# Causal stage: one block projected ahead, blocks taken as 0, 2, 3, 1, and zero products beside the first unit's maxima scores

## The chip, the core and the metric

The kernel runs on one core of one Trainium2 chip. A core has five engines with queues of their own: TensorE (PE, matrix products, with its weight loads shown as PEld), VectorE (DVE), ScalarE (ACT), GpSimd (POOL) and SyncE (SP, which issues DMAs here). Each takes its instructions in the order of its queue and waits for others by semaphores. The metric is device time in microseconds of one execution, and the median over runs is compared. TensorE's clock is granted by a throttle; the profile shows it as a share of full speed.

## What is computed

A model of four layers works on one sequence of 2048 tokens of width 128; layers are attention-like or feed-forward blocks, each added to the residual stream. The part that changes is the second attention of layer 0, causal attention with 16 heads of width 8 and rotary embedding. Reduced to what matters:

```python
q, k, v = heads(Wq, bq), heads(Wk, bk), heads(Wv, bv)
q = _apply_rope(q, cos, sin)
k = _apply_rope(k, cos, sin)
att = jnp.einsum('bhqd,bhkd->bhqk', q, k) * (1.0 / np.sqrt(D))
causal = jnp.tril(jnp.ones((T, T), bool))
att = jnp.where(causal[None, None], att, NEG_BIG)
att = jax.nn.softmax(att, axis=-1)
y = jnp.einsum('bhqk,bhkd->bhqd', att, v)
y = y.transpose(0, 2, 1, 3).reshape(B, T, C)
return jnp.einsum('btc,oc->bto', y, Wp) + bp
```

The result goes onto the residual stream, and a mixture-of-experts stage follows.

## The kernel before

Fourteen stages run one after the other (`STAGES`). Each works on the 2048 tokens as four blocks of 512 (`NB`, `BW`). The residual stream `x` stays on the chip. `Core.run` drives the stages as generators: while one stage's `main` runs, a `feed` opens the next stage and runs its first steps, block by block (`blocks`, `early`), as soon as the current stage says that it has room. A block is taken up only when the stage before has finished it: `before.final > b`. The attribute `own` says how many blocks a stage leaves for its own `main`; the first `NB - own` come ahead of it. What of the feed is not done when the stage before ends is run to its end there. The order of instructions on each engine comes from a scheduler that simulates the program, except that products of the Causal stage marked by `in_turn` keep the order in which the program issues them.

The Causal stage (`Attn16`, `Attention`):

- `early(b)` projects a block: layer norm (`normed`, `turned`), values into `at_V` (`project`), keys through `heads("k", b)` and four `slot` products into the transposed keys `at_KT`, one tile for each group of four heads. `heads` multiplies by the weights and by a rotated copy of them, loads the cosine and sine tables of the block (256 KB each, single buffers), multiplies by them on DVE, adds on POOL and splits the result into two parts for precise products. `heads("q", b)` does the same for the queries.
- Before, `own` is 1: blocks 0, 1 and 2 come ahead of the stage's `main`, then `main` projects block 0's queries. Block 3 is projected in steps (`tick`, `need`) between the scores.
- A unit is a pair of a head group g and a query block b; 16 units in the order of blocks 0, 1, 2, 3, four groups each. The last query rows' keys are those of blocks 0 to b, so the work of a unit grows with b + 1.
- `pass_a(u)` finds the row maxima: scores of two heads for 128 queries and up to 512 keys (L829), a mask on the diagonal (L832) and a maximum (L833), both on DVE. At the end of a unit the maxima are transposed (L850), copied (L852) and sent by DMA into the query tile (L854), so that later scores come out with the maximum subtracted.
- `pass_b(u)` computes the transposed scores by key tiles of 128 (L900, with the mask as a product, L903), exponentiates on ACT (L906) and multiplies by the values (L879), accumulating in the one PSUM bank `ps_c`. Beside these stand products with a tile of zeros (L883), which add nothing to the sums.
- The maxima of the next units run ahead of the exponential pass by six pairs of scores (`lead`), so that at a change of block the longer maxima of the new block stand beside the exponentials of the old one.
- `tail` and `out` normalise, project and add to the residual (L948) once all four groups of a block are done; `out` sets `final` to b + 1.

Of the kernel before, what the change touches and what calls it, by code (L numbers as in the profile page):

```python
# [15 lines left out]
BF16 = mybir.dt.bfloat16  # L16
# [5 lines left out]
P = 128  # L22
T = 2048
NT = T // P
NB = 4
# [7 lines left out]
class Core:  # L33
    def __init__(self, ctx, tc, ins):
        self.ctx, self.tc, self.nc, self.ins = ctx, tc, tc.nc, ins
        nc = self.nc
        self.per = ctx.enter_context(tc.tile_pool(name="per", bufs=1))
        self.x = self.per.tile([P, NT, P], F32, name="x")
        self.load_x(ins["x"])
        self.ident = self.per.tile([P, P], F32, name="ident")  # L40
        make_identity(nc, self.ident)
        self.identb = self.per.tile([P, P], BF16, name="identb")
        nc.vector.tensor_copy(self.identb, self.ident)
        self.identr = self.per.tile([P, P], F32R, name="identr")
        nc.vector.tensor_copy(self.identr, self.ident)
        self.ones = self.per.tile([P, P], F32, name="ones")
        nc.vector.memset(self.ones, 1.0)
        self.nhalf = self.per.tile([P, 4], F32, name="nhalf")
        nc.vector.memset(self.nhalf, -0.5)
        self.rev8 = self.per.tile([P, 4, E], F32, name="rev8")  # L50
        for e in range(E):
            nc.vector.memset(self.rev8[:, :, e : e + 1], float(E - e))
        self.neg01 = self.load(self.per, "neg01", (P, 1), ins["neg01"])
        slots = self.per.tile([P, 4, P], F32R, name="slots")
        with tc.tile_pool(name="st0", bufs=1) as st:
            nc.vector.tensor_copy(slots, self.load(st, "slots_raw", (P, 4, P), ins["slots"]))
        self.slots = {"q": (slots[:, 0], slots[:, 1]), "k": (slots[:, 2], slots[:, 3])}
        self.kone = self.load(self.per, "kone", (P, 1), ins["kone"])
        one = self.per.tile([2, 1], F32R, name="ones2")
        nc.vector.tensor_copy(one, self.ones[0:2, 0:1])  # L60
        self.ones2 = one.to_broadcast([2, BW])
        self.wide = self.per.tile([P, BW], BF16, name="wide")
        nc.vector.memset(self.wide, 1.0)
        self.zerob = self.per.tile([P, 32], BF16, name="zerob")
        nc.vector.memset(self.zerob, 0.0)
        self.psum = ctx.enter_context(tc.tile_pool(name="psum", bufs=1, space=PSUM))
        self.shared = {}
# [106 lines left out]
class Stage:  # L174
# [5 lines left out]
    own = 0  # L180
# [382 lines left out]
class Attention(Stage):  # L563
# [3 lines left out]

    pace = 12

    lead = 0.15  # L570

    halve, ahead = True, 0.35
    own = 2
    every = 1

    def start(self):
        self.have, self.count = NB - self.own, 0
        self.left = self.blocks(self.have, NB)

    apart = 4  # L580
# [23 lines left out]
    def units(self, scale):  # L604


        units = [(g, b, 0, 4) for b in range(NB) for g in range(4)]
        if self.halve:
            units[0:1] = [(0, 0, 0, 2), (0, 0, 2, 4)]
        preps = [u[:2] for n, u in enumerate(units) if u[2] == 0][1:]  # L610
        follows = {u: v[:2] for u, v in zip(units, units[1:]) if v[2] == 0}

        def astream():
            for n, u in enumerate(units):
                for p in self.pass_a(u):
                    self.tick()
                    if preps and p > self.ahead and preps[0] == follows.get(u):
                        self.prep(*preps.pop(0))
                    yield n + p
                yield n + 1.0  # L620

        sa = astream()
        pos = 0.0
        lead = lambda n: self.lead if self.lead < 1 else self.lead / self.pairs_of(units[min(int(n), len(units) - 1)])

        def advance(to):
            nonlocal pos
            while pos < to:
                pos = next(sa, 1e9)

        prev, at = iter(()), 0.15
        advance(1.0 + lead(1))
        for n, u in enumerate(units):
            for p in self.pass_b(u, scale):
                advance(min(n + 1 + p + lead(n + 1 + p), len(units)))
                if p > at:
                    next(prev, None)
                    at += self.gap
                yield
            for _ in prev:  # L640
                pass
            prev, at = self.finish(u), 0.15
        for _ in prev:
            pass
# [3 lines left out]
    def finish(self, u):  # L648
        self.tail(u)
        if u[0] == 3 and u[3] == 4:  # L650
            yield
            yield from self.out(u[1])


    pre = None

# [18 lines left out]

    def finish_late(self, u):
        while self.closed != u:
            if u == (3, NB - 1, 0, 4):
                self.later(2)
            else:  # L680
                yield
        yield from Attention.finish(self, u)


class Attn16(Attention):
# [38 lines left out]
    def early(self, b):  # L724
        xn = self.normed(b)
        yield
        ln = self.turned(xn)
        yield
        for _ in self.project(b, ln):
            yield  # L730

    def heads(self, which, b):
# [55 lines left out]
    def main(self):  # L788
        self.start()
        self.wk = self.pool("at_k", 2)  # L790
        self.qhl = self.heads("q", 0)
        self.prep(0, 0)
        self.banks()
        for b in range(self.have):
            add_bias(self.c, self.bo, b)
        self.roomy = True
        yield from self.units(self.scale)

    def prep(self, g, b):
        q = self.wk.tile([P, BW], F32R, name="at_q", bufs=self.NQ)  # L800
        self.slot(q, "q", g, self.qhl)
        if g == 3 and b + 1 < NB:
            self.need(b + 2)
            self.qhl = self.heads("q", b + 1)
        self.qb[(g, b)] = q

    def pass_a(self, u):

        c, nc = self.c, self.c.nc
        g, b, i0, i1 = u
        q, KT = self.qb[(g, b)], self.KT[g]
        mx = self.wk.tile([P, 4, 4, 4], F32, name="at_mx")
        nch = b + 1 if self.causal else 4
        steps = self.steps(u, nch)
        for n, (i, ch) in enumerate(steps):
            nk = P * (4 * b + i + 1) if self.causal else T
            w = min(BW, nk - ch * BW)
            diag = self.causal and ch == nch - 1  # L820
            self.need(ch + 1)
            left = [1, 0]
            while left:
                jj = self.pair if self.pair in left else left[0]
                left.remove(jj)
                pa = self.ps("a", (P, 2, BW))
                for k in range(2):
                    r = rows(2 * jj + k)
                    self.in_turn(nc.tensor.matmul(pa[:, k, :w], q[r, i * P : (i + 1) * P], KT[r, ch * BW : ch * BW + w], start=True, stop=True))  # L829
                if diag:  # L830
                    d = pa[:, :, w - P : w]
                    nc.vector.tensor_tensor(d, d, self.maskb.unsqueeze(1).to_broadcast([P, 2, P]), ALU.add)  # L832
                nc.vector.tensor_reduce(mx[:, i, 2 * jj : 2 * jj + 2, ch], pa[:, :, :w], AX.X, ALU.max)  # L833
                if n == len(steps) - 1 and not left:
                    self.due.append([2, u, self.set_max(lambda j: q[32 * j + 24 : 32 * j + 26], mx[:, :, :, 0:nch], i0, i1)])
                yield (n + 1 - len(left) / 2) / len(steps)

    def set_max(self, to, mx, i0=0, i1=4):
        c, nc = self.c, self.c.nc
# [21 lines left out]
    def pass_b(self, u, scale):  # L861
        c, nc = self.c, self.c.nc
        g, b, i0, i1 = u
        self.turn_due(u)
        q, KT = self.qb[(g, b)], self.KT[g]
# [3 lines left out]
        def av(kt, off, ps, half):  # L869
# [6 lines left out]
            for j in (3, 2, 1, 0):  # L876
                h = 27 * (4 * (g // 2) + j) + 9 * (g % 2)
                start, stop = kt == i0 == g % 2 == half == 0, kt == nkt - 1 and g % 2 == half == 1
                self.in_turn(nc.tensor.matmul(self.acc[32 * j : 32 * j + 32, s], self.V[:, kt, h : h + 32], ps[j][:, s], start=start, stop=stop))  # L879
            z = s if kt == 0 or end < BW else slice(half * BW // 2, (half + 1) * BW // 2)  # L880
            for j in (3, 2, 1, 0):
                if not (kt == nkt - 1 and half):
                    self.in_turn(nc.tensor.matmul(self.acc[32 * j : 32 * j + 32, z], c.zerob, c.wide[:, z], start=False, stop=False))  # L883
            if kt == nkt - 1 and half:
                self.closed = u
            if kt == nkt - 1 and g % 2 == half == 1:
# [48 lines left out]
    def out(self, b):  # L935
        c, nc = self.c, self.c.nc
# [9 lines left out]
            nc.tensor.matmul(po[:, i * P : (i + 1) * P], yT[:, i * P : (i + 1) * P], self.wt["o"], start=True, stop=True)  # L946
        xb = c.xb(b).rearrange("p t d -> p (t d)")
        nc.vector.tensor_tensor(xb, po, xb, ALU.add)  # L948
        self.final = b + 1


class Causal(Attn16):
    pre, causal, rope, halve = "l0b_", True, True, False
    own = 1
    lns = 4
    lnx = 1


class Attn2(Attn16):
    pre, halve, own = "l2b_", False, 1  # L960
# [3 lines left out]
class Filtered(Attn16):  # L964
    pre, halve, own = "l3b_", False, 1
# [341 lines left out]
class Mla(Attention):  # L1307
# [9 lines left out]
    own = 0  # L1317
# [199 lines left out]
    def out(self, b):  # L1517
        c, nc = self.c, self.c.nc
# [12 lines left out]
                nc.tensor.matmul(po[:, s], yT[:, k, s], self.F[:, k, :], start=(k == 0), stop=(k == 1))  # L1531
        xb = c.xb(b).rearrange("p t d -> p (t d)")
        nc.vector.tensor_tensor(xb, po, xb, ALU.add)
        self.final = b + 1


class Ssm(Stage):
# [271 lines left out]
class Hale(Attn16):  # L1809
# [41 lines left out]
    own = 0  # L1851
# [587 lines left out]
```

## Time and profile before

| | |
|---|---|
| runs | 4833.01, 4835.98, 4851.77 us |
| median | 4835.98 us |
| profiled execution | 4842.59 us, its span 4840.6 us |
| mean granted clock | 0.922 |
| Causal stage, first maxima score to last residual addition | 318.2 to 860.9 us |

The costliest groups of the stage, from 300 to 865 us of the profiled execution:

| line, engine, what | count | busy us | mean ns |
|---|---|---|---|
| L833 DVE maxima | 320 | 330.1 | 1062 |
| L906 ACT exponentials | 640 | 305.0 | 532 |
| L879 PE values | 2560 | 207.4 | 401 |
| L900 PE transposed scores | 640 | 181.4 | 505 |
| L829 PE scores for the maxima | 640 | 165.8 | 530 |
| L883 PE zero products | 1216 | 98.6 | 304 |
| L832 DVE masks | 128 | 54.2 | 427 |

Products overlap in the array, so that the busy times of PE's groups add up to more than PE's own. A stretch of the profile is named by its microseconds from the start of the span. In the answers by stretch, the columns are the length, the busy time of PE, PEld, DVE, ACT and POOL with the number of instructions in brackets, the granted clock, the share of the DMA engines and the GB/s moved.

### The profile page before, as it was taken

Reading aid. Unit: us, or ns where it says so; the run is one execution under the profiler, and the core shown is the slowest. Engines: PE = TensorE matmul, PEld = TensorE weight load, DVE = VectorE, ACT = ScalarE, POOL = GpSimd, SP = SyncE. Lnnn points to the kernel's source line nnn. Section 1 sums busy time; section 2 is a strip of 40 time slices with the busy share of each in tenths; the row PEclk is TensorE's granted clock in tenths of the full one; section 3 lists DMA queues with packets and bytes.
Section 4 is the critical chain, followed back from the end, with each engine's and each line's share of the span. In section 5 each row is a group of like instructions: output and inputs, shape, how many; then the busy total and the mean of one; then the engine's idle time right before and its main releaser. Section 6 shows DMA issues by size and latency. Waiting matters only on the chain.

```text
span 4840.6 us, 89173 instructions
## 1 busy us (share of the span) xinstructions
PE 4411.5 (91%) x36388; PEld 2496.4 (52%) x36388; DVE 3713.6 (77%) x5694; ACT 3052.4 (63%) x5570; POOL 947.6 (20%) x826
## 2 busy tenths in 40 slices
PE   6979999988799998799999999989988989999998
PEld 4744444655344443463444457656656634444466
DVE  7867886689666653789999958457768879999777
ACT  4634667775355555356888875345546648888876
POOL 4730000544100000330000013012215600000056
PEclk9966899998699999888999999889998969999999
DMA  1010000000000000000000000112211000000000
GB/s 52 6 45 6 4 2 9 22 1 17 17 14 14 18 14 4 8 1 2 2 2 2 2 4 12 33 50 51 51 48 37 9 8 2 2 2 2 2 20 7
DMA packets 69484, 73.33 MB, mean 15 GB/s; under 512 B 17616, under 2 KB 44102, under 8 KB 69076
## 3 DMA queue, kind: packets, MB, share of 16 engines
q1 hardware_dynamic: 69076, 67.64, 5.0%
q8 instruction: 287, 4.70, 0.4%
q14 instruction: 121, 0.99, 0.1%
HBM read 32.09 MB, written 1.05 MB: 7 GB/s over the span
## 4 chain that ended last, share of the span: by engine, by line
PE 68%; DVE 21%; ACT 5%; issue 3%; POOL 2%; DMA 1%; SPq 0%; POOLq 0%; ACTq 0%; DVEq 0%
PE ps_c L879 15%; PE ps_a L829 10%; PE ps_c L1483 5%; DVE at_mx L833 4%; PE ps_b L900 4%; PE ps_a L1443 3%; PE ps_c L883 3%; PE ps_b L1496 3%; PE ps_b L148 2%; PE ps_a L148 2%; PE ps_a L150 2%; PE ps_b L149 2%; PE ps_a L149 2%; PE ps_b L150 2%; DVE m_hl L455 1%
## 5 line engine op out<-in xcount | busy, mean ns | idle before, releaser
L906 ACT ACTIVATE at_P<-ps_b 128x512 f32<-128x512 f32 (+2 forms) x2688 | 1414.4, 581 | 335.0 <-PE ps_b L900 211.1
L833 DVE TENSOR_REDUCE at_mx<-ps_a 128x2 f32<-128x1024 f32 (+2 forms) x1344 | 1537.7, 1184 | 106.5 <-PE ps_b L900 66.8
L879 PE MATMUL ps_c<-at_P,at_V 128*32 128x256 f32 (+3 forms) x10752 | 868.3, 396 | 7.8 <-ACT at_u L888 7.3
L900 PE MATMUL ps_b<-at_q,at_KT 32*128 32x512 f32 (+2 forms) x2688 | 759.5, 499 | 6.6 <-DMA at_q<-at_mT 5.0
L829 PE MATMUL ps_a<-at_KT,at_q 32*128 32x512 f32 (+3 forms) x2688 | 701.1, 521 | 48.0 <-DVE at_mx L833 45.7
L829 PEld LDWEIGHTS ps_a<-at_KT,at_q 32*128 32x128 f32 x2688 | 267.1, 196 | 497.4 <-issue 338.1
L1444 DVE TENSOR_REDUCE ml_mx<-ps_a 128x2 f32<-128x1024 f32 x256 | 305.4, 1222 | 216.4 <-PE ps_a L1443 215.4
L454 ACT ACTIVATE m_hh<-ps_a,moe_b 128x512 fp32r<-128x512 f32 x512 | 349.8, 689 | 189.1 <-DVE m_h L451 158.0
L455 POOL TENSOR_TENSOR m_hl<-m_h,m_hh 128x512 fp32r<-128x512 f32 x256 | 360.5, 1409 | 541.1 <-ACT m_hh L454 529.3
L1498 ACT ACTIVATE ml_P<-ps_b 128x512 f32<-128x512 f32 (+1 forms) x544 | 272.5, 576 | 231.8 <-PE ps_b L1496 229.7
L879 PEld LDWEIGHTS ps_c<-at_P,at_V 128*32 128x32 f32 x10752 | 215.8, 110 | 359.2 <-issue 181.0
L883 PE MATMUL ps_c<-wide,zerob 128*32 128x256 bf16 x5184 | 391.1, 282 | 0.0
L266 POOL TENSOR_TENSOR ln_rs<-ln_ve,nhalf 128x4 f32<-128x4 f32 x56 | 61.8, 1104 | 1650.3 <-DVE ln_ve L264 1641.4
L900 PEld LDWEIGHTS ps_b<-at_q,at_KT 32*128 32x128 f32 x2688 | 326.3, 189 | 73.5 <-issue 44.2
L455 DVE TENSOR_TENSOR m_hl<-m_h,m_hh 128x512 fp32r<-128x512 f32 x256 | 257.1, 1005 | 79.4 <-ACT m_hh L454 77.9
L453 ACT ACTIVATE m_h<-ps_a,moe_b 128x512 f32<-128x512 f32 x320 | 220.6, 690 | 77.1 <-DVE m_hl L455 42.0
L1483 PE MATMUL ps_c<-ml_P,ml_V 128*33 128x512 f32 (+3 forms) x1088 | 257.5, 596 | 2.9 <-ACT ml_P L1498 2.9
L148 PE MATMUL ps_b<-m_hh,moe_w2h 128*128 128x512 f32 x512 | 221.7, 433 | 20.7 <-DVE m_t L475 17.8
L149 PE MATMUL ps_b<-m_hl,moe_w2h 128*128 128x512 f32 x512 | 213.9, 418 | 26.4 <-DVE m_hl L455 20.7
L148 PE MATMUL ps_a<-ln_h,moe_w1h 128*128 128x512 f32 x512 | 218.7, 428 | 10.7 <-ACT m_hh L454 10.6
L883 PEld LDWEIGHTS <-zerob 128*32 128x32 bf16 x5184 | 156.1, 100 | 113.6 <-issue 10.8
L149 PE MATMUL ps_a<-ln_l,moe_w1h 128*128 128x512 f32 x512 | 207.4, 405 | 0.0
(655 smaller groups left out, 7759.7 us busy)
## 6 DMA issues: line engine op xcount, KB each, us to landing
hl_KS<-hl_pkh SPq DMA_DIRECT2D x160, 64.0 KB
moe_w_raw<-in_l0f_W SPq DMA_DIRECT2D x32, 256.0 KB
ml_pad<-ml_QT SPq DMA_DIRECT2D x32, 256.0 KB
moe_w_raw<-in_l3f_W SPq DMA_DIRECT2D x32, 256.0 KB
hl_KS<-hl_pkl SPq DMA_DIRECT2D x80, 64.0 KB
at_pad<-at_q SPq DMA_DIRECT2D x64, 64.0 KB
at_q<-at_mT SPq DMA_DIRECT2D x192, 4.0 KB
at_cosT<-in_cosT SPq DMA_DIRECT2D x8, 256.0 KB
```

The source lines that it names most:

```text
L148: nc.tensor.matmul(out, lh, rh, start=start, stop=False)
L149: nc.tensor.matmul(out, lh, rl, start=False, stop=False)
L454: nc.scalar.activation(hh, ph, AF.Relu, bias=bias)
L455: (nc.gpsimd if f in ((0, 2) if self.spare else MS) else nc.vector).tensor_tensor(hl, h, hh.bitcast(F32), ALU.subtract)
L829: self.in_turn(nc.tensor.matmul(pa[:, k, :w], q[r, i * P : (i + 1) * P], KT[r, ch * BW : ch * BW + w], start=True, stop=True))
L833: nc.vector.tensor_reduce(mx[:, i, 2 * jj : 2 * jj + 2, ch], pa[:, :, :w], AX.X, ALU.max)
L879: self.in_turn(nc.tensor.matmul(self.acc[32 * j : 32 * j + 32, s], self.V[:, kt, h : h + 32], ps[j][:, s], start=start, stop=stop))
L883: self.in_turn(nc.tensor.matmul(self.acc[32 * j : 32 * j + 32, z], c.zerob, c.wide[:, z], start=False, stop=False))
L900: self.in_turn(nc.tensor.matmul(pbs[k][:, off:end], KT[r, kt * P : (kt + 1) * P], q[r, off:end], start=True, stop=not diag))
L906: nc.scalar.activation(p[:, off:end], pbs[k][:, off:end], AF.Exp, scale=scale)
L1444: nc.vector.tensor_reduce(mx[:, i, :, ch], pa, AX.X, ALU.max)
L1483: self.in_turn(nc.tensor.matmul(self.acc[64 * j : 64 * j + m, s], v, ps[k][j][:, s], start=kt + k == 0, stop=kt + k == NT - 1))
```

## The change

Three parts, all in the Causal stage. `own` goes from 1 to 3: only block 0 is projected ahead, and its queries belong to that projection; blocks 1, 2 and 3 are projected between the scores, where each gets its bias addition too (`prepared`). The blocks' units are taken in the order 0, 2, 3, 1; `final` counts up only over blocks that are finished without a gap. And while no unit is closed and no value product is pending, each pair of maxima scores is followed by two products of a 128x128 tile of zeros with a 128x512 tile of ones into `ps_c`; for this the zero tile grows from 32 to 128 columns, and the older zero products use its first 32. In the changed program 32 such products stand in PE's queue, between the score pairs of the first unit and of most of the second. The other stages' order of instructions stays, but for a few neighbours changing places.

```diff
-        self.zerob = self.per.tile([P, 32], BF16, name="zerob")
+        self.zerob = self.per.tile([P, P], BF16, name="zerob")
...
+    order = tuple(range(NB))
...
-        self.have, self.count = NB - self.own, 0
+        self.have, self.count, self.through = NB - self.own, 0, set()
...
-        units = [(g, b, 0, 4) for b in range(NB) for g in range(4)]
+        units = [(g, b, 0, 4) for b in self.order for g in range(4)]
...
+    def over(self, b):
+        self.through.add(b)
+        while self.final in self.through:
+            self.final += 1
...
-            if u == (3, NB - 1, 0, 4):
+            if u == (3, self.order[-1], 0, 4):
...
         for _ in self.project(b, ln):
             yield
+        if b == self.order[0]:
+            self.qhl = self.heads("q", b)
+            yield
...
         self.wk = self.pool("at_k", 2)
-        self.qhl = self.heads("q", 0)
         self.prep(0, 0)
...
-        if g == 3 and b + 1 < NB:
-            self.need(b + 2)
-            self.qhl = self.heads("q", b + 1)
+        if g == 3 and b != self.order[-1]:
+            b1 = self.order[self.order.index(b) + 1]
+            self.need(b1 + 1)
+            self.qhl = self.heads("q", b1)
...
                 nc.vector.tensor_reduce(mx[:, i, 2 * jj : 2 * jj + 2, ch], pa[:, :, :w], AX.X, ALU.max)
+                if self.closed is None and not self.late:
+                    self.warm()
...
+    busy = 0
+
+    def warm(self):
+        if self.busy:
+            pz = self.c.ps("c")
+            for _ in range(self.busy):
+                self.in_turn(self.c.nc.tensor.matmul(pz, self.c.zerob, self.c.wide, start=True, stop=True))
...
-                    self.in_turn(nc.tensor.matmul(self.acc[32 * j : 32 * j + 32, z], c.zerob, c.wide[:, z], start=False, stop=False))
+                    self.in_turn(nc.tensor.matmul(self.acc[32 * j : 32 * j + 32, z], c.zerob[:, 0:32], c.wide[:, z], start=False, stop=False))
...
-        self.final = b + 1
+        self.over(b)
...
 class Causal(Attn16):
     pre, causal, rope, halve = "l0b_", True, True, False
-    own = 1
+    own = 3
     lns = 4
     lnx = 1
+    order, busy = (0, 2, 3, 1), 2
```

The other attention stages keep `order` 0, 1, 2, 3 and `busy` 0.

More of the change, by code (lines that the diff above doesn't have):

```diff
@@ L1533, in out @@
         nc.vector.tensor_tensor(xb, po, xb, ALU.add)
-        self.final = b + 1
+        self.over(b)
 class Ssm(Stage):
```

## The prediction

> **What bounds the kernel now.** I read the page first, then a table of busy time by stretch of the Causal stage (marks: 281.0, where block 0's keys are done; 318.2, the first maxima product; then the moments at which a unit's or a block's maxima are copied out at L852, read off ScalarE's timeline; 856.3, the last unit's copy-out), then short windows of the clock, then the timeline.
>
> ```profile
> PE 4411.5 (91%) x36388; PEld 2496.4 (52%) x36388; DVE 3713.6 (77%) x5694; ACT 3052.4 (63%) x5570; POOL 947.6 (20%) x826
> ...
> PEclk9966899998699999888999999889998969999999
> ```
>
> TensorE (PE) is busy 91% of the span. The stage lies in slices 3 to 8, where the clock row shows its first 6.
>
> ```profile
> 281.00:318.20 37.20, 24.47 (x65) 13.44 (x65) 15.66 (x35) 11.75 (x19) 6.18 (x5) 0.58 0.28 86
> 318.20:340.40 22.20, 14.78 (x55) 7.56 (x54) 19.21 (x38) 4.78 (x8) 1.26 (x1) 0.50 0.07 24
> 340.40:388.00 47.60, 47.14 (x350) 21.55 (x354) 29.41 (x56) 18.97 (x46) 1.27 (x1) 0.50 0.04 13
> 388.00:415.80 27.80, 25.32 (x214) 12.10 (x210) 18.78 (x28) 8.96 (x25) 0.00 (x0) 0.56 0.01 2
> 415.80:503.80 88.00, 84.11 (x828) 39.00 (x828) 68.07 (x126) 48.91 (x104) 3.57 (x3) 0.74 0.03 8
> 503.80:534.40 30.60, 26.68 (x322) 12.49 (x318) 28.56 (x36) 16.94 (x40) 0.00 (x0) 0.97 0.01 2
> 534.40:638.60 104.20, 101.06 (x1214) 46.45 (x1213) 92.92 (x131) 73.71 (x153) 3.39 (x13) 0.91 0.02 5
> 638.60:676.90 38.30, 34.59 (x432) 15.89 (x428) 36.79 (x43) 24.92 (x54) 0.00 (x0) 0.99 0.01 2
> 676.90:813.20 136.30, 135.48 (x1609) 60.37 (x1605) 115.63 (x144) 98.95 (x199) 1.02 (x1) 0.88 0.01 2
> 813.20:856.30 43.10, 42.38 (x554) 19.51 (x547) 0.00 (x0) 35.31 (x75) 0.00 (x0) 1.00 0.07 21
> ```
>
> Columns: length, busy us of PE, weight loads, VectorE (DVE), ScalarE, GpSimd, then the clock. I call these rows S0 to S9; they sum to 575.3. Read four things. S0 holds no attention at all: blocks 1 and 2 and block 0's queries are projected while PE works 24 of 37 us at 0.58. In S2, the rest of block 0, PE is full (47.1 of 47.6) at half clock, and DVE is not (29.4). S3 and S5 are the passages to a longer block, and S5 is nearly all DVE. In S9 the last exponential pass runs alone, DVE empty.
>
> ```profile
> 375.00:380.00 5.00, 5.00 (x56) 2.34 (x54) 4.05 (x6) 1.98 (x6) 0.00 (x0) 0.50 0.01 3
> ...
> 438.15 0.79 PE L829 MATMUL ps_a<-at_KT,at_q 32*128 32x512 f32 x2
> 438.16 0.79 PE L900 MATMUL ps_b<-at_q,at_KT 32*128 32x512 f32 x2
> 438.88 1.08 PE L879 MATMUL ps_c<-at_P,at_V 128*32 128x256 f32 x8
> 439.74 0.44 PE L883 MATMUL ps_c<-wide,zerob 128*32 128x256 bf16 x4
> 440.11 0.71 PE L829 MATMUL ps_a<-at_KT,at_q 32*128 32x512 f32 x2
> ```
>
> The clock is 0.50 from 287.0 to 409.9, again to 440.6, then mostly 1.00. It moves in steps of 3.41 us. A PE without a gap does not lift it: 375 to 380 is full at 0.50. Products over all 128 rows and columns do. I counted, over the whole trace, the 3.41-us steps at 0.50 that hold hardly anything else: filled to 75% or more with such products, 19 of 19 are followed by full clock; filled to 41 to 74%, 13 of 23. At 440.6 it rises after a step of unmasked value products (L879), zero products (L883) and scores on all four row groups together.
>
> The page of the Trainium skill titled "TensorE: Matmul & The Clock Gate", section "What's actually happening", says that one window of about 3.4 us of sustained activity gives full clock, which speaks against the zero products, since PE is already busy after 344. The rows differ, so the measurement decides. If the page's plain rule held, the products would be added work only, and the sum would be that of rival A below.
>
> **The change, part by part.** New stretches, in the new order.
>
> *Start (S0).* Blocks 1 and 2 no longer come ahead of attention. What is left is block 0's queries: 306.2 (first bias product) to 318.2 is 12.0 us, placed at 281. S0 becomes 12, that is 25 less. Nothing is removed: the two projections go into the next stretch. Each issues rope-table loads of 256 KB on SP and one GpSimd add of 1.26 us per rope, in single buffers; GpSimd is 6% busy in S1, so I price both at nothing there. Uncovered, one rope chain is the 2.8 to 3.6 us wait for the cast in S0, three times some 10 us.
>
> *First maxima (S1).* DVE: 19.2 now, plus what leaves S0: 15.7 less four weight splits of the next stage (4 x 0.69) and the query rope's three passes (2.1), so 10.8, together 30. PE at half clock: 14.8, plus 24.5 less some 6.5 for the queries, so 18, plus 32 zero products (two for each of 16 score pairs) of 128x512; the same shape in bf16 takes 0.43 between starts at half clock, 13.7. Together 46.5. The zero products make more than half of a step a full-height product and the projections' weight products add to it, so I take the clock to rise after three steps: 10 us at half, then 36.5/2 = 18, so 28 on PE. DVE then decides: 30 at S1's own share (19.21/22.20) is 35. Ends: 33, and 48 if the clock stays (46.5 over 0.97). The products write the single ps_c bank, which nothing else uses before the first value product on the same engine.
>
> *Rest of block 0 (S2).* Half clock: 47.6. Full clock: PE 23.6, DVE 29.4/0.865 = 34. No zero products are added after the first unit closes, and this work has never lifted the clock by itself, so I take the middle, 41.
>
> *Block 0 to block 2.* 24 wide maxima beside only 4 key tiles: DVE decides as in S5, 28.6 busy of 30.6. I take 32; ends 31 and 36 (half clock).
>
> *Block 2 (S6)* 104.2, with its 17 us at half clock inside; 106, ends 104 and 115. *Block 2 to 3 (S7)* 38.3 and *block 3 (S8)* 136.3 are as before.
>
> *Block 3 to block 1 (new).* The maxima lead by 6 pairs: 6/32 of a unit at block 3, 6/16 at block 1. So S9 is 1.19 units of lone exponential pass in 43.1, 36.2 a unit. The new passage holds 0.19 + 0.62 = 0.81 units, 29.5, and PE also does 16 score pairs of some 0.3: 35, ends 34 and 38.
>
> *Block 1 last (S4).* 88.0 at clock 0.74. At full clock DVE's 68.1 at S6's share (0.892) is 76. It starts warm but has the same masked tiles: 80, ends 76 and 88.
>
> *End (S9).* 1.375 units of 8 tiles, at 36.2/2 = 18.1: 25, ends 24 and 26.
>
> The reordering by itself moves little: each passage costs about the longer of its two halves, and in units of a block's length 1+3+2+6+3+9+4+12+4 = 44 is also 1+3+3+9+4+12+4+6+2. What pays is the start and the clock.
>
> Sum: 12 + 35 + 41 + 32 + 106 + 38.3 + 136.3 + 35 + 80 + 25 = 540.6, against 575.3: 34.7 less. Lower ends: 12+33+34+31+104+38.3+136.3+34+76+24 = 522.6, 52.7 less. Upper ends: 12+48+47.6+36+115+38.3+136.3+38+88+26 = 585.2, 9.9 more. The profiled execution took 4842.6 (span 4840.6), so it would be 4808; the runs' median is 4836.0, so I forecast 4801.
>
> **The rivals.** *A, the zero products do not lift the clock* and are work only: every stretch at its upper end, 4836 + 10 = 4846. For it: 375 to 380, and steps of 59, 66 and 73% full-height products that stayed low. Against it: the 19 of 19, and half of the rest, with ten steps in S1's 35 us to try in.
>
> *B, slower: the half clock is carried into block 2.* The place is the passage to block 2: 24 maxima keep DVE full and PE thin, as in 388 to 415.8, where the clock fell back to 0.50 after one step. Block 2's units are PE-full: S6 has 101.1 of 104.2 at 0.91, 33.7 a unit, which is 61 at 0.50 against 34.7, so 26.6 for each unit that runs low. On top of A, with one unit: 4846 + 27 = 4873. It decides from there; on top of my forecast it takes three units, 34.7 less against 80 more. Against it: block 1 recovered at 440.6 within its first exponential pass, and block 2 has eight unmasked tiles a unit.
>
> *C, the head start is eaten* because the projections' chains queue in order on PE and DVE: S1 at 48 with full clock afterwards, 22 less, 4814. It falls short of what can be told from no change and counts with A.
>
> **How the numbers follow.** Differences under 0.5% (24 us) can't be told from no change. Forecast (24 to 53 less) 0.55; A and C 0.28; B 0.17. The forecast's own range is 4783 to 4812; A, B and C lie beyond it. The range reaches down below the lower ends and up past A, part of B left out: 4775 to 4855. Faster by over 24 us takes the clock to rise in S1 or S2 at least in part: 0.55; same 0.28; slower 0.17.
>
> **What would show it.** First maxima product near 293 instead of 318; the clock at 1.00 within some 10 us after it; the first exponential pass near 328; block 0's maxima done by about 369; DVE empty for some 25 us at the end instead of 46.6; everything after the stage early by the same amount. I am wrong if the clock row is 0.50 throughout 290 to 400, if block 2's first unit shows 0.50, or if the first exponential pass starts no sooner than 340.

## The result, and the profile after

The changed kernel takes 4869.14 us (median of 14 runs, 4848.86 to 4899.49), the kernel before 4840.67 beside it (14 runs). The ratio is 1.0062, 95% interval 1.0046 to 1.0078: slower by some 30 us, where 35 less had been forecast and 4855 was the top of the range. The profiled execution took 4882.1, its span 4880.0, the mean granted clock 0.915 (0.922 before).

From the page of the changed kernel: busy time by engine, and the clock by fortieths of the span.

```profile
PE 4452.2 (91%) x36398; PEld 2512.8 (51%) x36420; DVE 3707.2 (76%) x5694; ACT 3051.3 (63%) x5570; POOL 950.8 (19%) x826
...
PEclk9966896999689999797999999889998969999999
```

PE is busy 41 us more than before, with hardly more instructions. The Causal stage lies in slices 3 to 8 as it did. By stretch, with the columns of the prediction's table (length; busy PE, weight loads, DVE, ACT, POOL; clock); the marks are the first maxima product (300.0), the copies of the maxima, now at L873, and at the end the copy of the last unit's result (L909):

```profile
282.00:300.00 18.00, 11.12 (x30) 6.51 (x30) 9.15 (x23) 6.29 (x11) 4.71 (x6) 0.50 0.43 132
300.00:342.30 42.30, 37.98 (x130) 17.24 (x132) 27.81 (x55) 9.16 (x15) 5.17 (x4) 0.66 0.12 37
342.30:397.40 55.10, 52.98 (x367) 23.59 (x370) 33.01 (x59) 22.11 (x51) 1.27 (x1) 0.50 0.04 12
397.40:439.10 41.70, 33.66 (x246) 15.25 (x242) 28.60 (x35) 9.54 (x28) 0.00 (x0) 0.50 0.01 1
439.10:551.40 112.30, 106.68 (x1184) 49.20 (x1185) 92.58 (x148) 74.30 (x150) 4.59 (x14) 0.86 0.02 7
551.40:590.20 38.80, 35.09 (x436) 15.92 (x432) 36.31 (x43) 24.86 (x53) 0.00 (x0) 0.98 0.01 2
590.20:725.80 135.60, 132.44 (x1612) 59.31 (x1612) 117.96 (x141) 100.17 (x201) 1.28 (x1) 0.92 0.02 4
725.80:766.60 40.80, 40.47 (x401) 16.52 (x393) 20.06 (x28) 26.02 (x53) 0.00 (x0) 0.71 0.01 2
766.60:864.00 97.40, 93.96 (x957) 41.93 (x953) 60.85 (x88) 55.43 (x120) 0.00 (x0) 0.74 0.01 2
864.00:887.50 23.50, 23.39 (x328) 11.31 (x320) 0.00 (x0) 17.38 (x43) 0.00 (x0) 1.00 0.11 36
```

Two marks of the prediction's table are not such copies. 340.4, called the first copy-out, is the first score of the exponential pass (the copy stands at 337.9); 856.3 lies 0.9 us behind the copy of the last result (855.4). That first score comes at 345.5 in the change, and by this mark its second and third stretch are:

```profile
300.00:345.40 45.40, 40.82 (x136) 18.09 (x138) 29.47 (x57) 10.39 (x18) 5.17 (x4) 0.65 0.11 35
345.40:397.40 52.00, 50.14 (x358) 22.74 (x362) 31.35 (x57) 20.89 (x50) 1.27 (x1) 0.50 0.04 12
```

Set against the rows S0 to S9, in the order of the work, with these two for S1 and S2:

| from, to | before | forecast | after |
|---|---|---|---|
| first maxima product at | 318.2 | 293 | 300.0 |
| first score of the exponential pass at | 340.4 | 328 | 345.4 |
| rest of block 0 | 47.6 | 41 | 52.0 |
| passages 0 to 1 and 1 to 2, block 1 in the middle / passages 0 to 2 and 3 to 1, block 1 last | 146.4 | 147 | 179.9 |
| block 2 | 104.2 | 106 | 112.3 |
| passage 2 to 3 and block 3 | 174.6 | 174.6 | 174.4 |
| lone end | 43.1 | 25 | 23.5 |
| stage's last copy-out at | 856.3 | 821.6 | 887.5 |

Of the 25 us that the start was to bring, 18 are there at the first maxima product; at the first exponential score the change is 5 us behind the kernel before. The end is shorter by 20 us, where 18 were forecast; the passages, block 1, block 0 and block 2 take all of it back and 31 more. The other 7 or 8 us by which this execution is longer come behind the stage. Of the three signs by which the prediction was to be wrong two are there: block 2's first unit shows 0.50, and the exponential pass starts later than 340. The third, a clock of 0.50 throughout 290 to 400, is not.

Short stretches show the clock:

```profile
306.00:309.40 3.40, 3.40 (x11) 0.98 (x9) 1.62 (x3) 0.22 (x1) 1.26 (x1) 0.50 0.23 77
309.40:323.10 13.70, 12.03 (x57) 5.49 (x58) 13.03 (x26) 4.14 (x7) 2.64 (x2) 1.00 0.14 41
319.60:323.10 3.50, 1.97 (x12) 0.64 (x10) 3.50 (x8) 0.62 (x1) 1.26 (x1) 1.00 0.29 86
323.10:342.30 19.20, 16.89 (x54) 7.98 (x54) 9.64 (x20) 4.22 (x7) 1.26 (x1) 0.50 0.11 39
...
439.10:463.00 23.90, 22.98 (x155) 10.60 (x153) 11.52 (x15) 10.88 (x20) 0.00 (x0) 0.50 0.01 2
463.00:480.00 17.00, 15.59 (x201) 7.10 (x203) 16.27 (x32) 12.63 (x24) 2.30 (x2) 1.00 0.00 1
```

The clock rises at 309.4, behind a step (306.0 to 309.4) that holds two pairs of zero products and the last weight products of a late block's keys. It stays up for four steps, in which DVE is nearly full (13.03 of 13.70) and sets the pace; in the last of them, the line 319.60:323.10, PE works 1.97 us of 3.50 beside a full DVE. Then it is 0.50 for 140 us, from 323.1 to 463.0, through the whole passage to block 2 and into block 2's first unit: the mechanism of rival B.

### The profile page after: what moved, and what is told of

It is laid out like the page before. It is cut to its first block, busy times and chain, and to the rows that moved or that the text cites. A ratio compares the mean times of both kernels' runs of the same rounds, so it can differ in the third digit from the quotient of the medians.

```text
span 4880.0 us, 89208 instructions
## 1 busy us (share of the span) xinstructions
PE 4452.2 (91%) x36398; PEld 2512.8 (51%) x36420; DVE 3707.2 (76%) x5694; ACT 3051.3 (63%) x5570; POOL 950.8 (19%) x826
## 4 chain that ended last, share of the span: by engine, by line
PE 69%; DVE 20%; ACT 4%; issue 3%; POOL 2%; DMA 1%; SPq 0%; POOLq 0%; ACTq 0%; DVEq 0%
PE ps_c L900 15%; PE ps_a L839 10%; PE ps_c L1505 5%; DVE at_mx L843 4%; PE ps_b L921 4%; PE ps_c L904 3%; PE ps_a L1465 3%; PE ps_b L1518 3%; PE ps_a L148 2%; PE ps_b L148 2%; PE ps_a L150 2%; PE ps_a L149 2%; PE ps_b L149 2%; PE ps_b L150 2%; DVE m_hl L455 1%
## 5 line engine op out<-in xcount | busy, mean ns | idle before, releaser
L843 DVE TENSOR_REDUCE at_mx<-ps_a 128x2 f32<-128x1024 f32 (+2 forms) x1344 | 1540.0, 1184 | 139.8 <-PE ps_b L921 76.9
L927 ACT ACTIVATE at_P<-ps_b 128x512 f32<-128x512 f32 (+1 forms) x2688 | 1414.4, 581 | 352.2 <-PE ps_b L921 224.4
L900 PE MATMUL ps_c<-at_P,at_V 128*32 128x256 f32 (+2 forms) x10752 | 874.6, 399 | 7.8 <-ACT at_u L909 7.3
L921 PE MATMUL ps_b<-at_q,at_KT 32*128 32x512 f32 (+1 forms) x2688 | 763.3, 502 | 6.0 <-DMA at_q<-at_mT 4.3
L839 PEld LDWEIGHTS ps_a<-at_KT,at_q 32*128 32x128 f32 x2688 | 268.8, 197 | 500.4 <-issue 340.4
L900 PEld LDWEIGHTS ps_c<-at_P,at_V 128*32 128x32 f32 x10752 | 216.3, 110 | 361.2 <-issue 184.6
```

The source lines that it names most:

```text
L921: self.in_turn(nc.tensor.matmul(pbs[k][:, off:end], KT[r, kt * P : (kt + 1) * P], q[r, off:end], start=True, stop=not diag))
L927: nc.scalar.activation(p[:, off:end], pbs[k][:, off:end], AF.Exp, scale=scale)
```

## The experiments

Eleven other kernels and the changed one once more, each with runs of the kernel before beside it; none leaves out any part of the computation. The four sets of runs of the kernel before have means between 4841.9 and 4843.5 us. "Own" is the number of blocks that the stage leaves for itself, "zeros" the zero products per pair of maxima scores.

| kernel | own | order | zeros | ratio | 95% interval | half clock, us | at equal half clock, us |
|---|---|---|---|---|---|---|---|
| before | 1 | 0123 | 0 | 1 | | 758 | 4852.8 |
| order_only | 1 | 0231 | 0 | 1.0026 | 1.0010 to 1.0042 | 796 | 4854.7 |
| own_only | 3 | 0123 | 0 | 1.0014 | 0.9989 to 1.0040 | 788 | 4852.1 |
| zeros_only | 1 | 0123 | 2 | 1.0016 | 0.9994 to 1.0039 | 774 | 4856.6 |
| own_zeros | 3 | 0123 | 2 | 1.0018 | 0.9993 to 1.0043 | 777 | 4857.8 |
| own_order | 3 | 0231 | 0 | 1.0001 | 0.9988 to 1.0013 | 764 | 4852.5 |
| order_zeros | 1 | 0231 | 2 | 1.0001 | 0.9983 to 1.0019 | 747 | 4857.5 |
| busy1 | 3 | 0231 | 1 | 1.0040 | 1.0024 to 1.0056 | 803 | 4858.5 |
| the change | 3 | 0231 | 2 | 1.0062 | 1.0046 to 1.0078 | 812 | 4864.6 |
| after_again (the change) | 3 | 0231 | 2 | 1.0077 | 1.0049 to 1.0104 | 822 | 4869.1 |
| dose4 | 3 | 0123 | 4 | 1.0034 | 1.0020 to 1.0048 | 777 | 4864.5 |
| nat_hold | 1 | 0123 | held | 0.9992 | 0.9979 to 1.0005 | 668 | 4877.6 |
| order_hold | 1 | 0231 | held | 0.9979 | 0.9964 to 0.9993 | 644 | 4879.5 |
| own_order_hold | 3 | 0231 | held | 1.0006 | 0.9988 to 1.0024 | 678 | 4880.2 |

The last two columns are worked out from the runs: time at half clock is twice (1 - mean granted clock) times the whole program's span, averaged over a kernel's runs (4 to 14; the kernel before 99). One straight line through the runs of all kernels, with a height for each kernel, has a slope of 0.31 us for each microsecond at half clock; the last column is that height at 790 us. It is a fit and not an experiment: it says that the two go together, not which makes which. The two sets of the change, 4.5 apart in it, show how good it is. For the three "held" kernels, 110 to 150 us away from 790, it is drawn far beyond their own runs.

**One part at a time.** order_only, own_only, zeros_only and own_zeros take the changed kernel and set back these lines:

```diff
-    own = 3
-    order, busy = (0, 2, 3, 1), 2
+    own = 1                            (order_only, zeros_only)
+    order, busy = (0, 2, 3, 1), 0      (order_only)
+    order, busy = (0, 1, 2, 3), 0      (own_only)
+    order, busy = (0, 1, 2, 3), 2      (zeros_only, own_zeros)
```

> Only the order 0, 2, 3, 1 of the change; three blocks ahead as before, no zero products beside the maxima (block 0's queries are projected right behind its keys, ahead of blocks 1 and 2). Theory O (the order is the loss: the 24 maxima of block 2 behind block 0 keep the half clock, and block 1 runs low again at the end): slower than before by 20 to 45 us, with the half clock reaching past the first maxima of block 2 and a passage 0 to 2 of some 40 us. Theory P (the deferred projections are the loss): within 10 us of before. Theory Z (the zero products are the loss): the same.

> Only one block projected ahead; natural order, no zero products. Theory O: faster than before by 5 to 20 us, since the first maxima start some 18 us sooner and half of it is given back. Theory P: slower than before by 15 us or more, with block 0's maxima done later than 388. Theory Z: within 10 us of before.

> Only the 32 zero products beside the first maxima; three blocks ahead, natural order. Theory O and P: within 10 us of before, the clock up for some 10 to 15 us and down again once the products end. Theory Z: slower by 15 us or more.

> The change without its order: one block ahead and the zero products, blocks 0, 1, 2, 3. Theory O: faster than the changed kernel by 25 to 45 us and not slower than before. Theory P or Z: within 15 us of the changed kernel, that is some 15 to 30 us slower than before.

Measured: only the order by itself is slower beyond doubt, by 0.26%, and that at equal half clock is 2 us; it meets 38 us more of half clock. These 13 us are fewer than the 20 to 45 of theory O. The early start and the zero products alone can't be told from no change, and together (own_zeros) they can't either; own_zeros is some 20 us faster than the change, less than O's 25 and more than the 15 of P and Z. So none of the three theories has its part that carries the loss, and the head start is worth nothing that can be measured even in the old order. The three single excesses add up to 0.56%, close to the change's 0.62; the pairs, below, show that this sum is a coincidence. No run sets all three parts back at once, so the rest of the edit (block 0's queries projected ahead of the stage, the wider zero tile) has no price of its own.

zeros_only shows the zero products at their weakest. The columns are as above, then L857, the zero products, by itself, with 30 of the 32 in the first stretch:

```profile
313.80:348.70 34.90, 33.87 (x97) 12.68 (x96) 21.64 (x40) 5.36 (x9) 1.26 (x1) 0.50 0.04 16
348.70:396.00 47.30, 46.89 (x353) 21.20 (x356) 29.15 (x55) 19.34 (x47) 1.27 (x1) 0.50 0.04 13
```

```profile
313.80:348.70 34.90, 15.59 (x30) 2.05 (x30) 0.50 0.04 16
```

From the first maxima product on, PE is full (33.87 of 34.90), nearly half of that is zero products over the whole array (15.59), and the clock is 0.50 throughout.

That it rose in the change seems to have been a matter of half a microsecond. own_zeros has the same products there, its second pair of zero products at 306.76 and the change's at 306.81, and its clock stays at 0.50 until 443. At 0.43 us for each product of 128x512, the change's step from 306.0 holds 1.7 us of zero products and 0.8 of a late block's weight products, 73% of 3.41. In own_zeros the step begins at 306.6: 2.0 and 0.2 us, 63%. Both lie in the span of 41 to 74% in which the prediction had counted 13 rises in 23 steps.

**The dose, and the clock by itself.** dose4 is own_zeros with four products for each pair. nat_hold and order_hold drop these and put others where the trace shows the clock to fall, at the masked key tiles and among the first scores of the second block:

```diff
-    order, busy = (0, 1, 2, 3), 2
+    order, busy = (0, 1, 2, 3), 4       (dose4)
+    order, busy = (0, 1, 2, 3), 0       (nat_hold; order_hold with 0, 2, 3, 1; both with own = 1)
+    hold = True
...
                 pa = self.ps("a", (P, 2, BW))
+                if self.hold and g == 0 and b == self.order[1]:
+                    for k in range(2):
+                        self.in_turn(nc.tensor.matmul(pa[:, k], c.zerob, c.wide, start=True, stop=True))
...
+            if self.hold and kt >= 4 * b and not (kt == nkt - 1 and half):
+                for _ in range(2 if b < 2 else 1):
+                    self.in_turn(nc.tensor.matmul(self.acc[:, z], c.zerob, c.wide[:, z], start=False, stop=False))
```

> The change without its order, but four zero products beside each maxima pair instead of two. Theory Dose (two products fill only about half of a 3.41-us step at half clock, too little to lift it; four fill 80%): the clock rises within two or three steps of the first maxima and stays up until the first exponential pass, which starts 5 to 15 us sooner than with two products (354 from the span's start there), time 5 to 15 us below the change without its order. Theory Work (zero products are only added work, whatever their number): the first exponential pass starts some 10 us later still, time 5 to 15 us above it.

> The kernel before (three blocks ahead, order 0, 1, 2, 3, block 0's queries right behind its keys), with full-height zero products of 128x256 added into the value sums beside every masked key tile (two a half tile in blocks 0 and 1, one in 2 and 3) and two of 128x512 into the score bank ahead of each maxima pair of the passage from block 0. Theory Clock (the stage's early blocks are set by the half clock): half clock in the stage falls from 225 us to under 120, time 20 to 50 us below before. Theory Work: half clock stays near 225 us and the time rises by 10 to 30 us.

> The same products with the order 0, 2, 3, 1. Theory Clock (the order loses because its passages and block 1 run at half clock): within 10 us of the natural order with the same products. Theory Match (the order loses because the longer maxima and the shorter exponential passes no longer stand side by side, whatever the clock): 15 to 30 us slower than the natural order with the same products.

> The change without its zero products: one block ahead, order 0, 2, 3, 1. If the parts add up (order some 12 us, one block ahead some 7, zero products some 8): 8 us faster than the changed kernel, that is some 20 us slower than before. If the zero products matter only together with the order: within 4 us of the order alone, some 14 us slower than before.

Measured: with four products the clock is up from 309 to 340, and the first exponential comes 11 us sooner than in own_zeros (343.9 against 355.2, one profile each). So far theory Dose holds, but not its time: the whole is 0.34% slower than before, and not faster than own_zeros (0.18%, the intervals overlap). Over the runs its half clock is that of own_zeros, 777.

The held clock shows what the clock is worth. Half clock falls by 90 us in nat_hold and by 114 in order_hold, 28 and 36 us at the slope of 0.31, and the time by 0.08% (not beyond doubt) and 0.21%. For nat_hold that is 4 us, far from the 20 to 50 of theory Clock, though the half clock fell about as far as that theory asked (the stage's granted clock, 0.80 before, is 0.89); Work, with 10 to 30 us more, fails too. By the last column each pays some 25 us for its products (10 to 40 us for slopes of 0.22 to 0.41). In order_hold they are 168 products of 128x256 and 48 of 128x512; at the 0.43 us that one of 128x512 takes at half clock, so 0.21 at full, that is 168 x 0.107 + 48 x 0.21 = 28 us. Theory Match falls: order_hold isn't slower than nat_hold, so an order with block 1 last loses nothing when the clock is held. Some of its stretches, from the mark of block 0's maxima to the stage's last copy-out:

```profile
391.00:431.00 40.00, 35.54 (x296) 15.29 (x288) 28.43 (x35) 9.55 (x27) 0.00 (x0) 0.93 0.00 1
...
540.00:578.00 38.00, 35.77 (x439) 16.48 (x432) 35.65 (x42) 24.78 (x53) 0.00 (x0) 1.00 0.01 3
...
708.00:745.00 37.00, 36.66 (x412) 16.07 (x404) 20.36 (x28) 26.78 (x55) 0.00 (x0) 0.86 0.01 2
745.00:829.00 84.00, 82.28 (x986) 38.24 (x988) 60.16 (x87) 54.49 (x118) 0.00 (x0) 0.94 0.01 2
829.00:857.30 28.30, 27.65 (x358) 12.65 (x350) 0.00 (x0) 18.31 (x43) 0.00 (x0) 1.00 0.08 30
```

The passage to block 2, first row, takes 40.0 at a clock of 0.93, hardly less than the 41.7 at 0.50; but PE's 35.54 us hold some 10 us of the dense products, so what full clock alone would give isn't shown. The passages and the end are 40.0 + 38.0 + 37.0 + 28.3 = 143.3, before 27.8 + 30.6 + 38.3 + 43.1 = 139.8: with the order the work is shifted, not saved.

own_order, the change without its zero products, is as fast as the kernel before, 1.0001; neither of its two expectations, some 20 and some 14 us slower, held. So without the zero products the change doesn't lose its 30 us; and since own_zeros, without the order, doesn't either, the products cost that much only in company.

**Why they cost there.** own_order at 1.0001 against the change at 1.0062, but own_only at 1.0014 against own_zeros at 1.0018: what makes the products dear in the one and free in the other? busy1 halves them, order_zeros takes the early start away, after_again is the changed kernel once more, with a second profile, and own_order_hold has the two best versions in one:

```diff
-    order, busy = (0, 2, 3, 1), 2
+    order, busy = (0, 2, 3, 1), 1       (busy1)
...
-    own = 3
+    own = 1                             (order_zeros)
...
-    own = 1
+    own = 3                             (own_order_hold, from order_hold)
```

> The changed kernel with one zero product for each pair of maxima scores in place of two: 16 products, not 32. With none (own_order) the ratio was 1.0001, with two 1.0062. Theory Work and Clock, in proportion: half of the products' own time (16 x 0.43 = 7 us at half clock) and some of the longer half clock, ratio 1.002 to 1.004, half clock over the whole span 775 to 800 us. Theory Threshold (two are too much because the first unit's chain of products, maxima and late projections falls behind at two, not at one): ratio 0.999 to 1.001. Theory Clock alone (any number changes where the half clock falls, the number itself is nothing): 1.004 to 1.006.

> Order 0, 2, 3, 1 and two zero products for each pair, but three blocks ahead as before: the change without its start. Theory Pair (the products cost because of the order: they put off the late units, and the longer second block behind them takes that in its half clock): as much above order_only (1.0026) as the changed kernel is above own_order, so 1.007 to 1.010. Theory Projection (they cost because the changed kernel has blocks 1, 2 and 3 to project among the first scores, where products on PE stand in the projections' way; before there is only one): 1.003 to 1.005, as zeros_only stood 1.0016 above the kernel before. Half clock over the whole span above 800 us by Pair, 790 to 800 by Projection.

> The changed kernel once more, to see what of its one profile comes again. Theory Clock carried: the ratio 1.005 to 1.007, the clock again at 0.50 from before the first passage into the first unit of block 2 (to 450 us or later), passage and block 1's stretch again over 40 and over 90 us. Theory Luck (the profile fell on a bad draw of the clock, though the median is right): the same ratio, but the clock up before 440, block 1's stretch near own_order's 77 us, and the time lost spread elsewhere.

> One block ahead, order 0, 2, 3, 1, no zero products before the first value product, and the dense zero products of order_hold at the masked key tiles and at the second block's first scores. Theory Sum (start, order and hold do not depend on one another, as own_order against order_only, 0.9975 apart, says): order_hold's 0.9979 with the start's share on top, ratio 0.996 to 0.998, half clock over the whole span some 640 us, first maxima near 300. Theory Match (what the one does the other already does: one block ahead gains only because it is less time at half clock, which the dense products take away anyway): ratio 0.998 to 1.000, half clock 640 again. Theory Waste (the dense products fall into stretches that the projections now fill): above 1.000.

Measured: busy1 is at 1.0040, where the ranges of Work and Clock and of Clock alone meet, half clock at 803, just above the 800 of the first; Threshold (under 1.001) falls, the other two can't be told apart. order_zeros is at 1.0001 with a half clock of 747: both of its theories, with 1.003 and more, fall. Projection falls on the traces as well. own_zeros projects the keys of blocks 1, 2 and 3 among the same scores as the change (first weight product at 303.0, 322.1 and 342.3; in the change at 303.1, 316.6 and 334.2) and pays next to nothing for the zero products, 1.0018 against own_only's 1.0014. So the loss of 30 us needs all three parts together; why it does is not shown.

own_order_hold is at 1.0006: Sum and its 0.996 fall. The figure lies where Waste had it, above 1.000, and its interval takes in Match too; neither had the half clock, 678 for 640. At equal half clock it is level with order_hold (4880.2 and 4879.5), so that the early start adds no work there but half clock. order_hold stays the only kernel that is faster beyond doubt, by 0.07 to 0.36%.

after_again repeats the profile of the change almost to the microsecond up to block 1: the clock up at 309, down at 323, up at 463. Its ratio, 1.0077, lies a little above the 1.005 to 1.007 of both theories; of the two, Clock carried has the clock and the stretches right. Behind that the profiles part: block 1 takes 92.1 us and the lone end 34.7 at 0.60, where the change had 97.4 and 23.5 at 1.00. The lines of its passage, of the stretch after it and of its end:

```profile
397.10:438.80 41.70, 33.64 (x246) 15.26 (x242) 28.60 (x35) 9.53 (x28) 0.00 (x0) 0.50 0.00 1
438.80:551.10 112.30, 106.68 (x1184) 49.24 (x1185) 92.58 (x148) 74.33 (x150) 4.59 (x14) 0.86 0.02 7
...
858.30:893.00 34.70, 34.07 (x328) 14.26 (x320) 0.00 (x0) 17.91 (x43) 0.00 (x0) 0.60 0.07 25
```

What the clock does in block 0 goes with where its steps of 3.41 us fall. In own_order it rises at 350.5 for four steps, in the change it does not. The first two groups of eight value products (L900 in the changed program, L879 before) begin at 347.24 and 349.84 in own_order, at 352.28 and 354.88 in the change: 2.60 us apart in both, with the same products between them. By steps of the clock, L900 alone (length, PE, weight loads, clock), own_order and then the change:

```profile
347.10:350.50 3.40, 1.74 (x16) 0.40 (x16) 0.50 0.02 5
350.50:354.00 3.50, 0.30 (x4) 0.00 (x0) 0.99 0.02 5
```

```profile
350.40:353.80 3.40, 1.08 (x8) 0.20 (x8) 0.50 0.00 0
353.80:357.20 3.40, 1.08 (x8) 0.20 (x8) 0.50 0.00 1
```

In own_order both groups begin in one step and the next is at full clock. In the change the zero products have put them off by 5 us, they fall into two steps, eight products each, and neither lifts the clock.

The other profiles agree. The same two groups, 2.60 us apart, stand in all eleven profiles without the dense products, the kernel before among them. In four the clock is up right behind them (own_only, own_order, order_zeros, dose4): there the first group begins between 0.5 us ahead of a step's start and 0.1 us behind it. In the other seven it begins 0.4 to 2.6 us behind the start, and the clock stays at 0.50. Where a step starts differs from profile to profile, as at 306.0 and 306.6 above, so that the same program may draw either, though the change's two profiles drew nearly the same; delaying the groups moves them to another place of the step, good or bad.

own_order has its 14 us of full clock from 350.5, with PE busier than DVE (12.41 and 10.94 us of 13.70); the change has its 14 us from 309.4, where DVE is the bound. Block 0's maxima are done at 387 in the one and at 397 in the other; 7 of these 10 us arise behind the first exponential score (44.9 us from 341.8 in own_order, 52.0 from 345.4 in the change).

## Why the prediction was wrong, step by step

The step that failed, above all, is S1: "I take the clock to rise after three steps: 10 us at half, then 36.5/2 = 18, so 28 on PE", and with it "DVE then decides". The clock rose as early as that, but the step took for granted that it stays up. With the clock up, the scores and their zero products come no faster than DVE takes the maxima; in the last step at full clock PE works 1.97 of 3.50 us, and at 323.1 the clock is back at 0.50. S1 is 45.4, between the 35 taken and the upper end of 48.

The 35 wasn't there to be had in any case. own_order has no zero products to wait for, and its S1 (300.0 to 341.8) takes 41.8 us. DVE is busy 29.07 us in it, as forecast (30), but not at the share of 0.865 at which it was to decide: it waits 12.4 us for products and casts of the late blocks' projections. 8.9 of them belong to the chain of weight products, rope and cast, which was taken to be covered because GpSimd is only 6% busy. In own_zeros, where the clock never rises, S1 is 53.5 with PE busy 50.56, so that the 46.5 for PE at half clock and the upper end of 48 were too low as well.

*Start*, 12 forecast, is 18.0. PE waits 6.69 us there for the cast of the query rope (L142), where it waited 2.84 before: on ScalarE and DVE the rope now stands behind casts and splits of the next stage's weights, some of which wait for their DMA. So the first maxima product comes at 300.0 instead of 293, and the head start of 18 is used up before the first exponential score: rival C's step, which was given a place only beside a clock that then stays up.

S2, 41 forecast as the middle between half and full clock, is 52.0 at 0.50 throughout, beyond its own upper end of 47.6. That end was the old S2 at half clock; it left out that work of the start now stands here: the last two zero products, two products of a late block's keys, and 46 scores of the maxima for 42 then. PE is busy 50.14 us for 47.14, and its gaps are 1.4 us longer.

*Block 0 to block 2*, 32 forecast with 36 as the upper end, is 41.7 in the change, 41.6 in own_order and 40.0 in order_hold at a clock of 0.93. Here the mechanism was wrong: "DVE decides as in S5" is refuted by DVE's own timeline in the change, with the time that it waited and for what in brackets.

```profile
407.52 3.49 DVE L843 TENSOR_REDUCE at_mx<-ps_a 128x2 f32<-128x1024 f32 x3 [0.82 <-PE ps_a L839]
418.57 1.23 DVE L843 TENSOR_REDUCE at_mx<-ps_a 128x2 f32<-128x1024 f32 x1 [7.56 <-PE ps_a L839]
```

DVE waits 13.1 us of this stretch for the next scores, 7.56 of them at once; before, in S5, it waited 1.4. In order_hold the same wait is 11.5, with a longest one of 6.2. The scores stand in PE's queue in the order of issue, behind block 0's exponential pass, whose unit has only four key tiles to hand out 24 maxima over: from 409.6 to 417.7 PE runs that pass alone. Whether the clock has a share in it is open, since the passage is at 0.50 in every profile of this order without the dense products.

*Block 2*, 106, is 112.3, inside its ends: the clock is carried low into it, as 439.1 to 463.0 shows. Rival B's place, its mechanism and its half clock were right; its price, 27 us for a unit, was too high, because the clock came back within the first unit: 8 us over S6. That its 4873 lies close to the measured 4869.14 is luck. Against the upper ends of A the stage is 21 us longer, but block 2 is 3 us below its own; the 21 come from the start (7), block 1 (9), the two passages (9) and S2 (4), less what block 2, S1 and the end fall short of theirs.

*Passage 3 to 1*, 35 forecast, is 40.8 at 0.71; at full clock it is 31.4, in order_zeros and in busy1. *Block 1 last*, 80 with ends 76 and 88, is 97.4 at 0.74 and 92.1 in after_again; it is 77.0 at 1.00 in own_order and 84.0 at 0.94 in order_hold. So the prices of both at full clock were right or on the safe side, and the clock was not: block 1 starts warm, as forecast, but doesn't stay so; the clock was at 0.50 from 784 to 801, 808 to 832 and 845 to 856. Why own_order's is up there, with the same products in the same order, isn't shown; a draw of the steps, as in block 0, is likely, but each kernel but the changed one has a single profile.

What held: the end, 23.5 for 25, but only as long as the clock is up; it is 34.7 in after_again and 35.3 in own_order, both at 0.60, so that it held in this profile by luck. S7 and S8 held, 174.4 for 174.6, and so did "the reordering by itself moves little", 4854.7 and 4852.5 at equal half clock against 4852.8. *Start* and *order* were thus, by the fit, rightly judged to be no added work. The changed kernel's 29 us (4871.5 less 4842.9, the means of the runs) are by the fit 54 us more of half clock x 0.31 = 17, and 12 of work; 32 x 0.43 = 13.7 was the products' own time in S1. In the profiles much of the half clock is the stage's: from 281 to 900 the granted clock is 0.77 in the change and 0.82 before. Rival A had the 13.7 and took the clock to stay as it was; the runs show it worse than before.

Open: why the mean half clock is 812 with all three parts, 764 without the zero products and 747 without the early start. One or two profiles for each kernel show a mechanism and not how often it strikes. Not tried: zero products that stop before the first exponential, so that the value products aren't put off.

## What to carry to other kernels

Products that were added to raise TensorE's clock here raised it only until the array thinned out again, and at a place where another engine set the pace; the lift was lost there, and the products stayed as work. Even where they held the clock, they cost, by the fit, nearly what it brought. A price for a passage taken from a stretch in which one engine is full holds only if that engine's supply comes in the same rhythm: look at who feeds it there. Look at what a chain waits for, not at how busy its engine is: the rope chain was put at nothing because GpSimd was idle, and DVE waited some 9 us for the chain it belongs to. A part that costs nothing alone can cost in company, so leave one out of the whole besides trying one by itself.

## What the runs showed of the hardware

Half clock on a PE that is 91% busy cost 0.31 us per microsecond here, over all runs and kernels (0.22 to 0.41 within those with 11 runs or more). A microsecond at half clock holds half a microsecond of work at full clock, so that 0.50 is what it would cost if PE alone set the pace throughout; by the fit some three fifths of that were paid, and the rest lay under other engines' work or waits.

A full PE and a lifted clock are two things: 46.89 of 47.30 us at 0.50 in zeros_only, and 15.59 us of full-array zero products among 33.87 without a rise. The same two pairs of zero products were followed by full clock in the change and not in own_zeros, where the steps lay 0.6 us later. The page "TensorE: Matmul & The Clock Gate" of the Trainium skill, section "What's actually happening", has the throttle released after one busy window of about 3.4 us, and the window running freely, so that the same kernel differs from run to run. The steps of 3.41 us and the part that their position plays agree with these traces; that any busy window is enough doesn't.

Two profiles of one kernel can have their half clock at the same places within 0.6 us from 283 to 807, then part, and its runs still range over 50 us, from 4848.86 to 4899.49.
